# B11 of the merged weight evicted with the turned sign, and eleven x slots in the first stage of a two-layer graph kernel

## The chip, the cores and the metric

The kernel runs on one core of a Trainium2 chip, in fp32. The metric is the device time of one execution in microseconds (us), as the median of several executions. A separate execution is recorded by the hardware profiler; its times count from the start of its span. TensorE multiplies matrices, VectorE (DVE) and ScalarE (ACT) work element by element, GpSimd (POOL) does small operations and issues the stores here, and SyncE (SP) issues most loads.

## The reference

Two layers over a graph of N = 3327 nodes with D = 512 features. `x` is [3327, 512] and `adj` is a dense [3327, 3327] matrix:

```
h = relu(layernorm(x))
q, k, v = h @ Wq.T + bq, h @ Wk.T + bk, h @ Wv.T + bv
a = q @ k.T / sqrt(D) + adj + adj
x = x + softmax(a) @ v

h = relu(layernorm(x))
A2 = adj + eye(N)
dscale = diagonal(A2) ** -0.5
x = x + relu((dscale[:, None] * A2 * dscale[None, :]) @ (A2 @ h @ W.T))
```

## The kernel before, in words

The rows are padded to 3328, that is 26 row tiles of 128 (`NT`), paired as t and t + `HALF` (13 pairs). Wq and Wk are merged into one matrix M = Wq' Wk / sqrt(D), so that the scores are h M h' and k is never formed. All large products are done as a Strassen-Winograd scheme of seven block products in place of eight. For such a product the right operand is kept as four blocks and four combinations: `four_differences(b)` (line 177) makes b[4] = b[0] - b[1], b[5] = b[3] + b[4], b[6] = b[1] - b[3] and b[7] = b[2] - b[5], all on VectorE. b[0] itself is needed with its sign turned, so a negation of b[0] follows it.

The **first stage** (lines 266 to 380) is what the change touches:

- The loads: wq and the later x tiles are issued by SP, wk and three early x tiles by ScalarE's queue. `load_x` (line 272) takes the next slot of `x_ring` (line 269), a ring of SBUF slots, seven of them before. A slot is free again when the tile's normalised copy has been written.
- M: sixteen matmuls (line 305) into four PSUM banks, then eight copies with a scale by ScalarE (line 309), two column halves of each bank, into the blocks M[0] to M[3]; M[0] is made of the left halves of the first two banks. Then come the four differences on VectorE (lines 179 to 182) and the negation of M[0] on ScalarE (line 312), which has to wait until line 179 has read M[0].
- Each x tile, in `h_transposed` (line 314): BNStats and its aggregate on VectorE (`norm`, lines 193 to 197), the power -1/2 on GpSimd (line 199), a bias on VectorE (line 203), then h by a ScalarE activation (line 321), which frees the x slot. GpSimd stores h (line 322). TensorE transposes it in four blocks into one PSUM bank (line 325); the banks are used in turn, two of them. The bank of a tile of the lower half (i < HALF) is emptied by a ScalarE copy (line 328); that of a tile of the upper half by a ScalarE copy (line 330) and two VectorE additions (lines 331 and 332), which also form the combinations of the left operand in `hp`. The tiles of a pair follow each other. After a group of pairs two more additions (lines 333 and 334) form the rest.
- A small product of wk with the bias (line 371, 32 one-column matmuls) follows the first group's transposes in the text.
- `project_q` (line 336) then forms the queries from M and `hp`: chains of matmuls (line 345) whose results are taken out by ScalarE (line 350, the first value) and VectorE (line 353, what is added to it), and stored by GpSimd (line 360).

The instruction order of this stage is set by the framework's scheduler, which works from the program's text, data dependences and buffers; each engine then runs its list in order. In the order so built, the transposes of the first group stand among the products of the one before, and the first two loads of `adjT` blocks (line 416, 384 KB each), which belong to the next stage, stand on SP between the seventh and the eighth x tile. From the scores (line 452) on, the order is written out by hand.

The SBUF slots called `mid` are shared over the stages: 0 to 3 hold h tiles in the first stage (`n_ring`, line 270); in the score stage 0 to 7 hold adjacency blocks (`g_rings`), 8 and 9 sums of them (`o_ring`), 10 and 11 and 13 and 14 other sums.

Of the kernel before, what the change touches and what calls it, by code (L numbers as in the profile page):

```python
# [12 lines left out]
ALU = mybir.AluOpType  # L13
# [34 lines left out]
def graph_layers_kernel(  # L48
# [28 lines left out]
    nc = tc.nc  # L77
# [4 lines left out]
    scale = 1.0 / math.sqrt(D)  # L82
    E = D // 2
# [25 lines left out]
    def bank(k, name):  # L109
        return banks.tile([P, BW], F32, name=name, tag=f"bank{k}")  # L110

    def ring(*slots):

        turn = itertools.cycle(slots)

        def take(shape, name):
            kind, k = next(turn)
            return kind(k, shape, name)

        return take  # L120
# [53 lines left out]
        nc.vector.tensor_add(o[:, 2], o[:, 1], g[:, 0])  # L174
        nc.vector.tensor_add(o[:, 3], o[:, 2], g[:, 2])  # L175

    def four_differences(b):

        yield nc.vector.tensor_sub(b[4], b[0], b[1])
        yield nc.vector.tensor_add(b[5], b[3], b[4])  # L180
        yield nc.vector.tensor_sub(b[6], b[1], b[3])
        yield nc.vector.tensor_sub(b[7], b[2], b[5])
# [83 lines left out]
                Chain.before()  # L266
            Chain.before = None

    x_ring = ring(*((mid, k) for k in range(10, 15)), (half, 13), (half, 14))
    n_ring = ring(*((mid, k) for k in range(4)))  # L270

    def load_x(i, queue=nc.sync):
# [6 lines left out]
    def blocks(slots, name):  # L279

        return [b[:, k] for b in (half(j, [P, 2, 2, E], name) for j in slots) for k in range(2)]
# [3 lines left out]
    first = {}  # L285
# [7 lines left out]
    M = blocks(range(4, 8), "M")  # L293
# [8 lines left out]
    ps = [bank(k, "mm") for k in range(DC)]  # L302
# [3 lines left out]
                             start=c == 0, stop=c == DC - 1)  # L306
    for r in range(DC):
        for z in range(2):
            nc.scalar.mul(M[2 * (r // 2) + z][:, r % 2], ps[r][:, z * E : (z + 1) * E], scale)
    for _ in four_differences(M):  # L310
        pass
    nc.scalar.mul(M[0], M[0], -1.0)

    def h_transposed(k):

# [84 lines left out]
    def more_queries(n, qt):  # L400

        wd = Q[groups[n][0]]
        qt += [half(k, [P, 2, Q[0]], "qt")[:, :, :wd] for k in q_slots[n % 2][4:]]
        for _ in four_differences(qt):
            yield
        nc.scalar.mul(qt[0], qt[0], -1.0)
        yield
# [142 lines left out]
    with in_order(*(e.engine for e in (nc.vector, nc.tensor, nc.gpsimd, nc.sync))):  # L550
# [9 lines left out]
        k = len(steps)  # L560
# [144 lines left out]
    class Right:  # L705
# [31 lines left out]
        def make(self):  # L737
            own, r = self.own, self.r
            if r == "p5":
                nc.vector.tensor_sub(own, self.two[:, :, 0:E], self.two[:, :, E:D])  # L740
            if r == "p6":
                nc.vector.tensor_add(own, own, self.two[:, :, 0:E])
                nc.vector.tensor_sub(own, own, self.two[:, :, E:D])
                nc.gpsimd.dma_start(self.t2[:, 0 : 2 * self.n], self.b[:, 0 : 2 * self.n])
            if r in ("p7", "p4"):
                nc.vector.tensor_sub(own, own, self.one)
            if self.n == 2:
                for _ in four_differences([self.b[:, k] for k in range(8)]):
                    pass
# [187 lines left out]
    def number_of(g, r, s, t):  # L937
        return ((g * len(ORDER) + r) * 2 + s) * len(every) + t
# [5 lines left out]
    for g in range(3):  # L944
        for n, r in enumerate(ORDER):
            for t, e in enumerate(every):
                k = number_of(g, n, 0, t)
# [9 lines left out]
    for n, job in enumerate(jobs):  # L957
        k = k0 + n * (k1 - k0) // len(jobs)
# [17 lines left out]
    for g in range(2):  # L976
        k = number_of(g, 5, 1, 2)
# [6 lines left out]
    for (n, s, t), its in {  # L984
# [4 lines left out]
        for i, when in zip(its, (between, within)):  # L989
            if i is not None:  # L990
                k = number_of(2, n, s, t)
# [428 lines left out]
```

## Time and profile before

| what | value |
|---|---|
| time, median of 5 executions | 2215.72 us (2214.07 to 2220.13) |
| the profiled execution: its own time | 2218.74 us |
| its span | 2217.0 us |
| its mean granted TensorE clock | 0.994 |
| TensorE busy in the span | 2178.9 us (98%) |
| ScalarE, at the negation (line 312), ahead of the last two M evictions: wait for VectorE | 4.78 us, ended 24.59 |
| x tiles 1 to 7 landed | 8.07 to 14.23 us |
| x tiles 8 to 11 issued, landed | 15.30 to 17.41, 18.16 to 22.59 us |
| x tiles 12 to 15 issued, landed | 27.25 to 31.54, 30.05 to 36.46 us |
| the last x tile landed | 61.17 us |
| first score product (line 452) | 122.0 us |

The table is read like this. The span is the profiled execution as the hardware recorded it; its own time lies 1.7 us above the span and 3.0 us above the median. TensorE's busy share says that it is at work nearly all the time. The three rows on x tiles come from following each load from its issue to its landing: between 17.41 and 27.25 SP issues no x tile. The granted clock of TensorE is full except for 24.35 to 31.18, 1997.25 to 2004.08, the start, and the tail from 2205.47 on, where it is half.

### The profile page before, as it was taken

To read this page: it belongs to the slowest core of one execution; us is meant where nothing else is said; L and a number is where in the kernel's file an instruction comes from. 1 tells how busy PE (TensorE), PEld (TensorE's weight loads), DVE (VectorE), ACT (ScalarE), POOL (GpSimd) and SP (SyncE) were. 2 spreads that over 40 slices of the span, in tenths; PEclk is the share of its full clock that TensorE was granted. 3 is DMA by queue.
4 is the path that set the end of the run, shared out by engine and by line. 5 is a ranking of instruction groups with operands and counts; after the bars stand their busy time and mean duration, and the time that the engine had idled before them with its cause. 6 is when DMAs were issued, how large, how long until landed. Compare 5 with 4: busy or idle time off the path is not lost.

```text
span 2217.0 us, 20976 instructions
## 1 busy us (share of the span) xinstructions
PE 2178.9 (98%) x6268; PEld 1167.7 (53%) x6268; DVE 1627.9 (73%) x3103; ACT 231.6 (10%) x336; POOL 356.1 (16%) x551
## 2 busy tenths in 40 slices
PE   9999999999999999999999999999999999999997
PEld 5555555455545555555454555555545555555554
DVE  6369888888877788877777778886645358776776
ACT  5312111211110000000001000000000000000011
POOL 4223333333331000001222100000000000000001
PEclk9999999999999999999999999999999999999998
DMA  7658888888969898788787999876645458765685
GB/s 250 213 203 299 293 302 284 299 285 310 351 208 322 308 371 310 273 295 310 259 304 262 312 340 355 281 275 200 215 140 188 131 185 305 236 201 178 208 302 170
DMA packets 246682, 583.68 MB, mean 263 GB/s; under 512 B 34768, under 2 KB 106270, under 8 KB 246558
## 3 DMA queue, kind: packets, MB, share of 16 engines
q1 hardware_dynamic: 192270, 399.28, 54.3%
q0 software_dynamic: 44928, 167.49, 19.9%
q10 hardware_dynamic: 9360, 15.47, 2.2%
q8 instruction: 52, 0.85, 0.2%
q14 instruction: 72, 0.59, 0.1%
HBM read 414.28 MB, written 167.85 MB: 263 GB/s over the span
## 4 chain that ended last, share of the span: by engine, by line
PE 89%; DVE 4%; DMA 3%; issue 2%; POOL 0%; ACT 0%; SPq 0%; ACTq 0%; POOLq 0%; DVEq 0%
PE p L780 53%; PE Y L452 12%; PE p L872 8%; PE Z L452 6%; PE p L772 5%; PE X L452 3%; PE Y L345 2%; DMA xt<-in_x_dram 1%; DMA g<-in_adjT_dram 1%; PE Z L345 1%; DVE part L173 1%; PE pt L925 0%; PE X L345 0%; DMA xr<-x1d 0%; DVE part L174 0%
## 5 line engine op out<-in xcount | busy, mean ns | idle before, releaser
L780 PE MATMUL p<-part,b 128*128 128x448 f32 (+1 forms) x3528 | 1255.0, 514 | 6.1 <-DVE part L174 4.9
L780 PEld LDWEIGHTS p<-part,b 128*128 128x128 f32 x3528 | 669.1, 190 | 571.4 <-issue 309.0
L173 DVE TENSOR_TENSOR part<-part 128x896 f32<-128x896 f32 (+1 forms) x252 | 257.0, 1020 | 93.5 <-PE p L780 48.6
L452 PE MATMUL Y<-qt,hp 128*128 128x448 f32 (+1 forms) x832 | 309.3, 514 | 4.8 <-DVE g L456 3.8
L452 PEld LDWEIGHTS Y<-qt,hp 128*128 128x128 f32 x832 | 157.0, 190 | 140.9 <-issue 72.3
L452 PE MATMUL Z<-qt,hp 128*128 128x384 f32 (+1 forms) x416 | 162.6, 513 | 0.0
L175 DVE TENSOR_TENSOR part<-part,part 128x448 f32<-128x448 f32 (+1 forms) x219 | 129.5, 591 | 16.6 <-DVE part L174 0.5
L174 DVE TENSOR_TENSOR part<-part,part 128x448 f32<-128x448 f32 (+1 forms) x219 | 129.4, 591 | 7.4
L772 PE MATMUL p<-part,b 128*128 128x448 f32 (+1 forms) x336 | 124.2, 513 | 0.0
L872 PE MATMUL p<-w,ct 128*128 128x512 f32 x272 | 123.5, 593 | 0.5 <-DVE part L884 0.4
L452 PEld LDWEIGHTS Z<-qt,hp 128*128 128x128 f32 x416 | 78.8, 190 | 67.4 <-issue 37.3
L456 DVE SCALAR_TENSOR_TENSOR g<-g,Y 128x384 f32<-128x384 f32 (+1 forms) x156 | 91.3, 585 | 29.3 <-PE Y L452 27.2
L866 POOL DMA_DIRECT2D sum<-job x52 | 28.4, 547 | 501.7 <-DVE job L863 283.1
L809 DVE TENSOR_TENSOR part<-p,part 128x384 f32<-128x384 f32 (+1 forms) x33 | 19.3, 586 | 107.9 <-PE p L780 107.1
L772 PEld LDWEIGHTS p<-part,b 128*128 128x128 f32 x336 | 63.6, 190 | 53.7 <-issue 32.4
L808 ACT COPY part<-p 128x384 f32<-128x384 f32 (+1 forms) x33 | 16.6, 502 | 683.4 <-PE p L780 682.4
L872 PEld LDWEIGHTS p<-w,ct 128*128 128x128 f32 x272 | 51.5, 190 | 59.8 <-issue 51.9
L452 PE MATMUL X<-qt,hp 128*128 128x384 f32 (+1 forms) x208 | 81.1, 513 | 0.0
L459 ACT ACTIVATE g<-g 128x768 f32<-128x768 f32 (+1 forms) x48 | 43.0, 896 | 354.4 <-DVE g L456 300.5
L444 POOL DMA_DIRECT2D sum<-o x52 | 36.9, 709 | 222.1 <-DVE o L438 151.9
L872 PE MATMUL p<-w,part 128*128 128x512 f32 x144 | 65.7, 592 | 0.0
L92 POOL DMA_DIRECT2D out_dram<-r x30 | 16.2, 542 | 305.3 <-DVE r L928 270.2
(166 smaller groups left out, 1879.1 us busy)
## 6 DMA issues: line engine op xcount, KB each, us to landing
part<-sum SPq DMA_DIRECT2D x104, 448.0 KB, 4.9
part<-p SPq DMA_DIRECT2D x91, 448.0 KB, 6.3
part<-sum SPq DMA_DIRECT2D x104, 384.0 KB, 3.5
part<-p SPq DMA_DIRECT2D x91, 384.0 KB, 4.1
part<-in_adjT_dram SPq DMA_DIRECT2D x78, 448.0 KB, 4.7
b<-row SPq DMA_DIRECT2D x234, 128.0 KB, 4.9
part<-in_adjT_dram SPq DMA_DIRECT2D x78, 384.0 KB, 3.8
g<-in_adjT_dram SPq DMA_DIRECT2D x52, 448.0 KB, 4.7
```

The costliest lines, as they stand in the source:

```text
L173: nc.vector.tensor_add(o[:, 0:2], g[:, 0:4:3], g[:, 1:2].to_broadcast([P, 2, g.shape[-1]]))
L174: nc.vector.tensor_add(o[:, 2], o[:, 1], g[:, 0])
L175: nc.vector.tensor_add(o[:, 3], o[:, 2], g[:, 2])
L345: nc.tensor.matmul(ps[:, :w], M[B[name]][:, c, o * P : (o + 1) * P], hp[k][:, A[name], c], start=start and c == 0, stop=c == 1, skip_group ...
L444: nc.gpsimd.dma_start(self.to(sumd)[:, 0:2], self.o)
L452: nc.tensor.matmul(ps[:, :wd], h_of(self.t, name, k), qt[B[name]][:, k], start=start and k == 0, stop=k == 1, skip_group_check=True)
L456: nc.vector.scalar_tensor_tensor(a[n], a[n], 2.0, ps[:, :wd], op0=ALU.mult, op1=ALU.add if sign > 0 else ALU.subtract)
L459: nc.scalar.activation(g[1], g[1], AF.Exp, **({"bias": pad} if self.t == HALF - 1 else {}))
L772: yield nc.tensor.matmul(ps[("p2", "p3", "p4", "p8")[k]][:, :w], b[:, z], a[:, 0, y], start=k == 3, stop=True)
L780: yield nc.tensor.matmul(ps[r][:, :w], b[:, i], m, start=self.t == 0, stop=self.t == PAIRS - 1 and r in ("p1", "p5", "p6", "p7"))
L866: nc.gpsimd.dma_start(sumd[self.s][self.j][:, 2 + self.k], self.a)
L872: nc.tensor.matmul(ps, cts[s][y][d][:, k * P : (k + 1) * P], w[d], start=d == 0, stop=d == DC - 1)
```

## The change

`four_differences` gets an argument with which it leaves out b[4]. The ring of x slots takes four slots more, `mid` 6 to 9, and so has eleven. The two evictions that form M[0] are scaled by -scale, so that M[0] is written with its turned sign at once. M[4] = M[0] - M[1] is then made from the turned block in one VectorE instruction, (M[0] * -1) - M[1], ahead of the other three differences, which don't read M[0]. The separate negation on ScalarE is gone.

```diff
-    def four_differences(b):
-
-        yield nc.vector.tensor_sub(b[4], b[0], b[1])
+    def four_differences(b, first=0):
+
+        if first == 0:
+            yield nc.vector.tensor_sub(b[4], b[0], b[1])
         yield nc.vector.tensor_add(b[5], b[3], b[4])
...
-    x_ring = ring(*((mid, k) for k in range(10, 15)), (half, 13), (half, 14))
+    x_ring = ring(*((mid, k) for k in range(6, 15)), (half, 13), (half, 14))
...
-            nc.scalar.mul(M[2 * (r // 2) + z][:, r % 2], ps[r][:, z * E : (z + 1) * E], scale)
-    for _ in four_differences(M):
+            turned = -scale if r < 2 and z == 0 else scale
+            nc.scalar.mul(M[2 * (r // 2) + z][:, r % 2], ps[r][:, z * E : (z + 1) * E], turned)
+    nc.vector.scalar_tensor_tensor(M[4], M[0], -1.0, M[1], op0=ALU.mult, op1=ALU.subtract)
+    for _ in four_differences(M, 1):
         pass
-    nc.scalar.mul(M[0], M[0], -1.0)
```

No further line differs. "Rows used one a step in another order", in the short description of the change, has no line of its own: the order changes only as the scheduler builds it from these edits. In the order so built:

| engine | what stands differently |
|---|---|
| ScalarE | eight M evictions in a row; before, the negation stood between the sixth and the seventh |
| VectorE | M[4] stands behind the BNStats of the 15th x tile; before, behind that of the 11th; the additions of the first pair (lines 331, 332) follow the differences of M in both |
| SP | the first adjacency load stands behind x tile 11, the second behind tile 15; before, both stood ahead of tile 8 |
| GpSimd | the powers (line 199) stand a little earlier among the stores of h |
| TensorE | three neighbouring groups change places (products of line 345 and transposes) |
| all, from the scores on | the same |

## The prediction

> **What bounds the kernel now.** I read the page's totals first, then TensorE's waits in the first stage, its timeline, and windows for the transfers and the clock. All times are us from the span's start; tiles of x are counted in the order of their loads.
>
> ```profile
> PE 2178.9 (98%) x6268; PEld 1167.7 (53%) x6268; DVE 1627.9 (73%) x3103; ACT 231.6 (10%) x336; POOL 356.1 (16%) x551
> ```
>
> TensorE is idle for 2217.0 - 2178.9 = 38.1 us in all. The change keeps the count and shapes of the matmuls, so it can only move idle time or the time in which the clock is halved. It edits the first stage alone, and behind that stage the two programs' instruction orders are the same on every engine. So only TensorE's gaps up to the first score product (L452, 122.0) count:
>
> ```profile
> PE tp L325 <- ACT hp L328: 2.7, 2, 2.0
> PE tp L325 <- DVE hp L332: 2.2, 2, 1.7
> PE Z L345 <- DVE hp L331: 0.9, 1, 0.9
> PE Y L345 <- ACT qs L350: 0.8, 1, 0.8
> PE tp L325 <- ACT ht L321: 0.2, 1, 0.2
> ```
>
> (The columns are total us, times, longest.) They sum to 6.8 us, which is the most that removed waits can bring. The first is the wait that the change aims at. The timeline shows its cause:
>
> ```profile
> 23.88 0.68 DVE L179 TENSOR_TENSOR M<-M 128x512 f32<-128x512 f32 x1
> 24.59 0.63 ACT L312 ACTIVATE M<-M 128x512 f32<-128x512 f32 x1 [4.78 <-DVE M L179]
> ...
> 25.66 0.59 ACT L328 COPY hp<-tp 128x512 f32<-128x512 f32 x1
> ...
> 26.30 1.12 PE L325 MATMUL tp<-ident,ht 128*128 128x128 f32 x4 [1.98 <-ACT hp L328]
> ...
> 27.94 0.41 DVE L332 TENSOR_TENSOR hp<-hp,tp 128x256 f32<-128x256 f32 x1
> ...
> 28.09 1.97 PE L325 MATMUL tp<-ident,ht 128*128 128x128 f32 x8 [0.68 <-ACT hp L328]
> ```
>
> The reader is to see a chain. ScalarE stands at the negation of M[0] (L312), which waits for M[4] on VectorE (L179), which stands behind the BNStats of the 11th x tile (landed 22.59). Behind L312 queue the last two M evictions and the copy that empties the first transpose bank, so TensorE has no bank from 24.3 to 26.30, then again for 0.68. The later gaps have x tiles behind them:
>
> ```profile
> 36.19 0.91 PE L345 MATMUL Z<-hp,M 128*128 128x384 f32 x2 [0.88 <-DVE hp L331]
> ...
> 62.69 0.63 PE L325 MATMUL tp<-ident,ht 128*128 128x128 f32 x4 [1.75 <-DVE hp L332]
> ```
>
> In the first, L331 (35.73) stood behind a BNStats whose tile landed at 35.10; in the second, L332 (62.13) stood behind two whose tiles landed at 60.09 and 61.17. Between 22.59 and 30.05 no x tile lands at all: all seven slots are full and ScalarE, which frees them (L321), is stuck.
>
> **The change part by part.**
>
> *The turned sign and the missing negation.* ScalarE loses one 0.63 us instruction and a 4.78 us wait. All eight evictions now follow one another: the sixth ended at 19.81, two more take about 0.65, so L328 of the first tile runs when its transposes are done (about 20.9) and ends near 21.5. Tile 3's transposes then start when TensorE is through with its bias products, at 24.31, not 26.30: **1.99 us earlier**. The next four, for tile 5 in the same bank, move with them (28.09 to 26.10). They end at 27.08 at the half rate of these records (1.97 for eight, so 0.98 for four).
>
> *M[4] as a scalar_tensor_tensor.* It takes the place of one tensor_sub of 0.68. The nearest row is L884, the same kind on 128x512 reading PSUM, 0.75; the other end is 0.68. I take 0.68; the 0.07 does not show.
>
> *Eleven slots.* Four more x tiles are loaded before any slot is freed. The program order on SP changes: x tiles 8 to 11 go ahead of both adjacency loads (384 KB each, issued at 10.63 and 11.12 before), the first of these follows tile 11, the second tile 15; no later instruction needs them before 87 us. Tiles 12 to 15, issued at 27.25 to 31.54 before, now wait for the first four slots, freed when tiles 8 to 11 were issued before (15.30 to 17.41). On VectorE there is a price: M[4], and with it L331/L332 of the first pair, stand behind the BNStats of the **15th** tile in place of the 11th. Queued behind it are the other three differences and these two additions; waiting for them is TensorE, for the second bank (tile 4).
>
> So when does tile 15 land? The windows of the transfers and of the clock:
>
> ```profile
> core 0: us, PE busy (x) PEld busy (x) DVE busy (x) ACT busy (x) POOL busy (x), PEclk, DMA share, GB/s
> 17.30:23.20 5.90, 5.90 (x39) 4.42 (x37) 3.21 (x12) 2.06 (x7) 2.89 (x6) 1.00 0.85 324
> ...
> 20.94:24.35 3.41, 3.37 (x31) 3.29 (x30) 2.28 (x10) 0.00 (x0) 0.00 (x0) 1.00 0.46 179
> 24.35:27.77 3.42, 1.12 (x4) 0.72 (x4) 2.18 (x5) 2.95 (x7) 0.25 (x1) 0.50 0.00 0
> 27.77:31.18 3.41, 3.09 (x10) 2.41 (x11) 1.75 (x7) 2.91 (x6) 2.40 (x5) 0.50 0.63 196
> ...
> 1997.25:2000.67 3.42, 2.35 (x4) 1.28 (x5) 3.32 (x8) 0.47 (x1) 0.00 (x0) 0.50 0.61 227
> ```
>
> At 16.29 before had landed all its early loads, 0.79 MB of adjacency among them. After has four x tiles and one adjacency block in their place, 1.44 MB; the extra 0.65 MB costs 2.0 us at 324 GB/s, so this lot is in at about 18.2. Then come four x tiles and four row stores (L322), 2.1 MB or 6.5 us: 24.7 for the last of them. In before the last of these eight was a store, 0.62 behind the last tile (23.21 against 22.59), so tile 15 lands at about **24.0**. Here the Trainium skill bears (DMA: Bandwidth & Descriptors, "Anatomy of one DMA"): a fixed 2.0 us plus bytes over 436 GB/s. By that rate the extra costs 1.5 and the lot 4.8, and tile 15 is in near 22.0; L332 would then be done before TensorE wants the bank, and the front gain would be the full 1.99. The row, taken with reads and stores mixed, decides: 324. The page's section "Issuing engines are not separate DMA queues" warns in the same direction: transfers of all issuers interleave on 16 engines, so more slots bring no bandwidth, only an earlier start. The trace has room for one: the row at 24.35 shows a DMA share of 0.00.
>
> From the landing, by the distances of before: 0.98 from that BNStats to M[4], 0.61 for each of M[4] and three differences, 0.33 to L332, 0.41 for it: 24.0 + 0.98 + 2.44 + 0.33 + 0.41 = 28.1. Tile 4's transposes start at 28.1 against 29.07 (28.09 + 0.98): **0.97 us is gained at the front**, not 1.99. That is one us for each us of tile 15, nought at a landing of 25.0.
>
> From there x tiles are issued four tiles earlier. Tiles came some 1.6 us apart (27.25 to 55.72 for 15 of them is 1.9), so 6 us or more of lead stands against waits of 1.75 at the most. So the gaps at 36.19 (0.88), 54.52 (0.15), 57.94 (0.42) and 62.69 (1.75) go: **3.20 us**. What is late next is the drain by ScalarE and VectorE; VectorE was busy 9.25 of 10 between 40 and 50, where TensorE did not wait. The 0.78 at 100.2 waits for L350, not for x, and stays.
>
> *The clock.* The half rate at 24.35 to 31.18 lies in before although TensorE was busy 3.37 of the 3.41 ahead of it: those are the bias product's one-column matmuls, which after has too. The Trainium skill (TensorE: Matmul & The Clock Gate, "What's actually happening") lets a free-running 3.4 us window decide, idle to half, busy to full. If after's window from 24.35 counts as busy, full rate returns at 27.77 and about 1.6 us more is gained (3.1 us of work at half rate). But after fills it with only 1.12 + 0.98 = 2.1 of 3.41, and the row at 1997.25 had 2.35 and left the clock at half. So by the row: no gain. The next window, 28.1 to 31.18, has 3.08, as 3.09 before, and is enough. If L332 ends later than 28.8 it holds under 2.35, and the half rate lasts to 34.6: up to 1.7 lost.
>
> *The slots' later use.* The slots added now hold x until the last L321, near 79; the adjacency and sum tiles that share them are written from 84 on (VectorE L438 at 87.85). The cover is 5 us or more; each us beyond it would cost up to one.
>
> **Sum.** 0.97 + 3.20 = 4.2 us. Against the profiled execution, 2218.74, that is 2214.5; the median before, 2215.72, is 3.0 lower, and I subtract from it: **2211.5**.
>
> **Rivals.**
> - *Everything fits* (0.15): tile 15 lands by 23, nothing waits at 27, the clock comes back early. 1.99 + 3.20 + 1.6 = 6.8: 2208.9. For it: share 0.00 in the middle of the stall. Against it: 324 GB/s.
> - *A new wait in the old one's place* (0.22): tile 15 lands at 25 to 26.5, L332 ends at 29 to 30.6. The front gives 0 to -1.5, the clock loses up to 1.7; with 3.20 later the sum is between +3 and 0: about 2214. For it: VectorE's order, and reads that meet stores.
> - *Slower* (0.13): transfers move at 236 GB/s (the last column), as in a later window of the same stage:
>
> ```profile
> 40.00:50.00 10.00, 10.00 (x38) 6.11 (x37) 9.25 (x32) 6.06 (x11) 5.59 (x10) 1.00 0.71 236
> ```
>
>   From 15.3 some 3.0 MB are left, tile 15 lands at 28, tile 4 starts at 32.1: 3.0 lost, clock 1.7 lost, and if row stores hold back the later tiles too, only half of the 3.20 comes: 3.1 slower, 2218.8. It decides from a landing of tile 15 near 27.
> - *No effect* (0.05): the x gaps return because stores, not slots, set the pace of loads (tile 14 was issued right at a store's landing, 30.57): within 1 of 2215.7.
>
> The forecast's own case has 0.45 and a range of 2209.5 to 2213.5. The range for 8 in 10 runs from 2207.0 to 2217.3, with the medians' own scatter (2214.07 to 2220.13). A measurement of this kernel tells some 0.2% (4.4 us) from no change, and 4.2 lies just at that bound: of the forecast's case I give half to each side. Faster by over 0.2%: 0.23 + 0.14 + 0.05 of luck in the phase of the clock's windows, 0.42. Slower by over 0.2%: that rival with a second clock window lost (another 1.7), 0.07, and 0.05 for the same luck the other way: 0.12. Within: 0.46.
>
> **What would show it.** Right: no ScalarE wait between the evictions; tile 3's transposes at 24.3; tile 15 landing near 24 and L332 ending near 28; no TensorE gap at 36, 58 or 62; L452 starting near 118. Wrong: tile 15 landing after 26, half rate past 31.2, or VectorE still waiting for x after 40.

## The result, and the profile after

| | before | after |
|---|---|---|
| median of the timed executions | 2217.58 us (44, 2213.78 to 2221.93) | 2212.62 us (23, 2206.51 to 2217.66) |
| profiled execution, its span | 2217.0 us | 2208.2 us |
| ratio after to before | | 0.9978, 95% interval 0.9972 to 0.9985 |

The change makes the kernel 4.9 us faster (0.0022 of 2217.6; by the interval 3.3 to 6.2). 4.2 were forecast. From here on a gain "by time" is 1 minus the ratio, times 2217; the difference of two medians can lie 1 us beside it. The spans of the two profiled executions differ by more, 8.8 us, and most of that is not the change. I cut each trace at the end of the merged weight's matmuls (line 305 before, 306 after) and at the first score product (line 452, 454): 19.97 and 121.86 before, 18.67 and 117.44 after. So 1.3 us lie ahead of the end of these matmuls (the last section says what this end goes with), 3.1 in the first stage behind it, and 4.4 behind the stage, where nothing is edited.

The page's totals of after:

```profile
PE 2175.5 (99%) x6268; PEld 1167.0 (53%) x6268; DVE 1627.6 (74%) x3103; ACT 230.9 (10%) x335; POOL 357.1 (16%) x551
```

TensorE's idle time is 2208.2 - 2175.5 = 32.7 us, against 38.1. Its waits between 20 and 130 in after (total us, times, longest):

```profile
PE Y L347 <- ACT qs L352: 1.1, 1, 1.1
PE tp L327 <- DVE hp L334: 0.9, 1, 0.9
PE tp L327 <- ACT hp L330: 0.7, 1, 0.7
PE tp L327 <- DVE nb L204: 0.7, 1, 0.7
```

They sum to 3.4 us; before they were 6.8. The wait of 2.0 for ScalarE's copy is gone, and so is the wait for VectorE's addition at 61 (1.75). One wait is new at the front, for L334. The one at 54.5, put down to L204, stands ahead of the 18th group of transposes, as the 0.42 of before at 57.94 does. The timeline of after around the front:

```profile
21.99 0.68 DVE L194 BATCH_NORM_STATS2 st<-xt 128x6 f32<-128x512 f32 x1
22.59 0.67 DVE L312 SCALAR_TENSOR_TENSOR M<-M 128x512 f32<-128x512 f32 x1
22.87 0.64 PE L327 MATMUL tp<-ident,ht 128*128 128x128 f32 x4
...
23.54 0.58 ACT L330 COPY hp<-tp 128x512 f32<-128x512 f32 x1 [2.72 <-PE tp L327]
...
24.18 0.87 PE L327 MATMUL tp<-ident,ht 128*128 128x128 f32 x4 [0.68 <-ACT hp L330]
...
25.51 0.41 DVE L334 TENSOR_TENSOR hp<-hp,tp 128x256 f32<-128x256 f32 x1
...
25.98 1.11 PE L327 MATMUL tp<-ident,ht 128*128 128x128 f32 x4 [0.94 <-DVE hp L334]
```

ScalarE has no negation to stand at; it waits for TensorE now. M[4] (L312) comes right behind the BNStats of the 15th tile, which landed at 21.78, and the first pair's last addition, L334, behind the differences. TensorE stands 0.94 us for it: this is the wait that takes part of the old one's place. Of the prediction's signs of being right, those of the front came, all a little earlier than named (tile 3's transposes at 22.87, the 15th tile at 21.78, L334's end at 25.92), and the gaps at 36 and 62 are gone; the one at 58 is not. Of its signs of being wrong, the half rate reaches just past 31.2 (31.32), and VectorE waits for no x tile after 40.

### The profile page after: what moved, and what is told of

Same layout as the page of the kernel before. It is cut to its first block, busy times and chain, and to the rows that moved or that the text cites. A ratio compares the mean times of both kernels' runs of the same rounds, so it can differ in the third digit from the quotient of the medians.

```text
span 2208.2 us, 20973 instructions
## 1 busy us (share of the span) xinstructions
PE 2175.5 (99%) x6268; PEld 1167.0 (53%) x6268; DVE 1627.6 (74%) x3103; ACT 230.9 (10%) x335; POOL 357.1 (16%) x551
## 4 chain that ended last, share of the span: by engine, by line
PE 87%; DVE 4%; issue 3%; DMA 3%; POOL 1%; ACT 0%; SPq 0%; ACTq 0%; POOLq 0%; DVEq 0%
PE p L782 52%; PE Y L454 12%; PE p L874 7%; PE Z L454 6%; PE p L774 5%; PE X L454 3%; PE Y L347 1%; DMA xt<-in_x_dram 1%; DMA b<-row 1%; DVE part L173 1%; PE pt L927 0%; DMA p<-g 0%; DVE part L174 0%; DMA xr<-x1d 0%; PE tot L507 0%
```

## The experiments

A single profile says little here, since the same kernel's gaps differ from one execution to the next. So the kernel before, the changed kernel and each of its two parts were profiled twice. In this table, d is the time from the end of the merged weight's matmuls to the first score product; idle is the part of it in which no matmul ran; clock is half of the matmul time that fell into stretches of half clock, that is, about what the half clock cost.

| kernel | d | idle | clock | windows of 3.41 at half rate | ratio to before (95%) |
|---|---|---|---|---|---|
| before | 101.9, 101.1 | 6.6, 4.1 | 2.1, 4.3 | 2, 3 | |
| after | 98.8, 96.8 | 3.4, 1.5 | 3.0, 3.1 | 2, 2 | 0.9978 (0.9972 to 0.9985), 0.9978 (0.9968 to 0.9988) |
| sign alone | 98.5, 101.4 | 3.0, 4.0 | 3.1, 4.8 | 2, 3 | 0.9988 (0.9979 to 0.9997), 0.9989 (0.9979 to 0.9999) |
| slots alone | 101.9, 100.9 | 5.0, 4.3 | 4.4, 4.1 | 3, 3 | 0.9987 (0.9980 to 0.9994), 0.9990 (0.9981 to 0.9999) |
| M first | 96.7, 98.3 | 1.4, 2.8 | 3.1, 3.1 | 2, 2 | 0.9969 (0.9957 to 0.9981), 0.9979 (0.9970 to 0.9989) |
| wide bias | 100.3 | 5.7 | 1.7 | 1 | 0.9987 (0.9980 to 0.9994) |
| M first, wide bias | 97.9 | 4.5 | 0.0 | 0 | 0.9970 (0.9958 to 0.9982) |
| M first, split bias | 95.1 | 2.2 | 0.0 | 0 | 0.9973 (0.9963 to 0.9983) |
| the same, queries later | 94.5 | 2.0 | 0.0 | 0 | 0.9972 (0.9960 to 0.9984) |

Idle time and clock can stand in for each other: where the half rate falls into the bias product, that product takes longer and TensorE comes later to the wait behind it. So the second profile of before has 2.6 us less idle time than the first, but 2.2 more lost to the clock, and d is only 0.8 shorter.

### Each part alone

Theory: the sign takes away ScalarE's stall at the front, the slots take away the later waits for x tiles, and the two add up. Rival: both cure one lack, loads of x that don't start while ScalarE is stuck, so either alone brings nearly everything. The sign alone is the changed kernel with

```diff
-    x_ring = ring(*((mid, k) for k in range(6, 15)), (half, 13), (half, 14))
+    x_ring = ring(*((mid, k) for k in range(10, 15)), (half, 13), (half, 14))
```

and the slots alone are the kernel before with the opposite edit. Expected of the sign alone:

> The turned sign and the scalar_tensor_tensor, with seven x slots as before (M[4] stands behind the BNStats of the 11th tile again). If the two parts add up, this gives the front alone: tile 3's transposes 2 us earlier, tile 4's about 1 us earlier, and the gaps at 36, 58 and 62 that wait for x stay: about 1.0 us faster than before, ratio 0.9995. Rival, that the parts cure the same lack (no x tile is loaded while ScalarE is stuck, so freeing ScalarE alone lets the loads run 4 us earlier): the later x gaps go too, about 3.5 us faster, ratio 0.9984.

Again, beside the changed kernel:

> The turned sign alone once more (seven slots), for a second profile and beside e7 on one chip. Idle up to the first score product 3.0 us with the 1.8 us gap at 58 if what e1 showed is no chance; time within 0.5 us of e7 if the slots add nothing on top of the sign, 2 us above it if they do.

> The changed kernel once more, for a second profile and beside e8 on one chip. Additive parts: 2 us faster than e8 (the slots take the 0.42 and 1.75 us waits for late x tiles). Substitutes: within 0.5 us of e8. TensorE idle up to the first score product 3.4 us, as in the first profile.

TensorE's waits between 20 and 125 in the first profile of the sign alone:

```profile
PE tp L327 <- DVE hp L334: 2.2, 2, 1.8
PE tp L327 <- ACT hp L330: 0.7, 1, 0.7
```

The 2.2 us are the gaps at 55 and 58 (0.42 and 1.80; in the second profile 0.42 and 1.69), the 58 and 62 of before. They stay without the slots, and no wait for L334 stands at the front: there M[4] is behind the 11th BNStats, and L334 is in time. Both profiles of the changed kernel have one gap of 0.67 instead, at the place of the first. Only the second of the two waits for a late x tile. VectorE in before, ahead of the first and then of the second:

```profile
56.46 0.16 DVE L203 SCALAR_TENSOR_TENSOR nb<-mv,rstd 128x1 f32<-128x1 f32 x1 [2.09 <-POOL rstd L199]
```

```profile
60.11 0.69 DVE L193 BATCH_NORM_STATS2 st<-xt 128x6 f32<-128x512 f32 x1 [1.25 <-DMA xt<-in_x_dram]
```

By time the sign alone is 2.7 and 2.4 us faster than before, and on one chip the changed kernel's median is 3.0 us below that of the sign alone (2212.58 against 2215.59; 2.4 by the two ratios). The 1.0 us that the theory gave the sign were missed: what was measured lies between this and the rival's 3.5. The 3.4 us of idle time expected of the changed kernel's second profile were missed as well (1.5).

Expected of the slots alone:

> Eleven slots with the separate negation kept (before's M code). If the parts add up: the x gaps go (2.3 us by the trace of after) but ScalarE still stands at the negation until M[4], which now comes behind the 15th BNStats: the front is not earlier, or up to 1 us earlier as tile 15 landed at 21.8; 2.3 to 3 us faster, ratio 0.9988. Rival, the parts cure the same lack: nearly all of the change's gain, 4 us or more, ratio 0.9981.

Again:

> Eleven slots alone once more, for a second profile and more times. Additive parts: 2.8 us faster than before, 2 us slower than the changed kernel. Idle up to the first score product 5 us, and a half rate of two windows instead of the three of e2 if the third there was chance.

TensorE's waits between 20 and 125 in the first profile of the slots alone:

```profile
PE Y L345 <- ACT qs L350: 1.5, 1, 1.5
PE tp L325 <- ACT hp L328: 1.4, 2, 0.8
PE tp L325 <- DVE hp L332: 1.3, 1, 1.3
PE tp L325 <- DVE nb L203: 0.7, 1, 0.7
```

Of the gaps at 58 and 62 only 0.67 is left, at the place of the first, but the front keeps its wait for ScalarE's copy (0.77, and 1.45 in the second profile; 1.98 and 0.90 in the two profiles of before) and a wait at 36 (1.34 and 0.77). This one has a late x tile behind it, with eleven slots:

```profile
34.94 0.69 DVE L193 BATCH_NORM_STATS2 st<-xt 128x6 f32<-128x512 f32 x1 [2.29 <-DMA xt<-in_x_dram]
...
36.43 0.63 PE L325 MATMUL tp<-ident,ht 128*128 128x128 f32 x4 [1.34 <-DVE hp L332]
```

The sign alone has no gap there, and VectorE in it waits for no x tile between 33 and 57. With the slots alone no x load is issued from 16.53 to 25.86, where ScalarE stands at the negation and frees no slot. So the lateness near 35 goes with ScalarE's stall and not with the number of slots: here the rival is right. By time the slots alone are 2.9 and 2.2 us faster than before. Three windows at half rate, in place of the two expected, came in the second profile too.

So some 2.5 for the sign, 2.2 to 2.9 for the slots, and 4.9 for both: the times favour the parts that add up. Each interval is about 2 us wide to either side, so the rival's 3.5 for one part alone is not excluded by one run, but the 3.0 us between the changed kernel and the sign alone on one chip speak against it, and so do the gaps: the wait for the negation and the lateness near 35 go with the sign, the wait for x near 60 with the slots. The length of the stage does not show it. By the means of two profiles d is 101.5 before, 100.0 with the sign, 101.4 with the slots and 97.8 with both: the slots' idle time is 0.7 us less than before, but the half clock took 1.0 us more. Over the timed runs it does not: their mean granted clock (0.9943 and 0.9946) is that of before beside them (0.9945 and 0.9943). Where the slots' 2.2 to 2.9 us lie is therefore not shown by these profiles.

### Which gaps were there by chance

> The kernel before once more, for a second profile. If its first-stage gaps are those of its order: idle 6 to 7 us up to the first score product with the gaps of 2.0 at 24, 0.7, 0.9 at 36 and 1.75 at 61; two or three windows at half rate. If they are chance, the places differ by over 1 us.

In the second profile of before the gaps at 24 (0.90), 26 (0.68), 56 (0.41) and 60 (1.72) stand at their places, and the one at 36 (0.88 in the first) is absent, though nothing was changed. It was a gap of that execution. The 2.0 at 24 also has a chance part: 0.90 here, where the half rate began at 22.61 inside the bias product and this product took 4.21 us in place of 3.63. The expectation of 6 to 7 us idle was missed: 4.05.

### The new wait: M first

If the wait for L334 is what is left of the old stall, putting M[4] to M[7] and the first pair's additions ahead of the 12th tile's BNStats should remove it. On the changed kernel, with an order-only dependence on VectorE:

```diff
+            rstd, bias = norm(xt, stats_behind) if j > 11 else norm(xt)
...
+        for ins in ahead:
+            tc.add_manual_dep(nc.cur_bb.bb.instructions[-1], ins.name,
...
```

where `ahead` holds the four M instructions and line 334's instruction of the second tile, and `stats_behind` is called right after a BNStats is issued.

> The changed kernel, with M[4] to M[7] and the first pair's two additions put ahead of the BNStats of the 12th x tile on VectorE (order only). If the new wait behind the 15th BNStats is what is left of the old one, the 0.94 us gap at tile 4's transposes goes (the 0.68 us wait for ScalarE's copy stays): 0.9 us faster than the changed kernel, 5.5 to 6 than before, and up to 1.6 more if TensorE's window from 24.3 then counts as busy and the clock comes back at 27.8. Rival, that delaying four BNStats starves the later transposes: no gain, ratio as the changed kernel, 0.9978.

> M first once more, as e3 had six times only. If the wait behind the 15th BNStats costs what the first profile of the changed kernel showed (0.94), 1 us faster than the changed kernel, ratio to before 0.9973 to 0.9965; if it is mostly absent, as in the second profile, the changed kernel's time.

The wait for L334 at the front is gone in both profiles. But it is gone in the second profile of the changed kernel too, where the bias product ran partly at half clock (4.64 us instead of 3.63) and tile 3's transposes later and slower (1.09 instead of 0.64), so that L334 at 25.45 was in time for 26.5. On average this order gains nothing that its 16 runs can show beside the changed kernel: medians 2212.05 and 2212.39 against 2212.62 and 2212.58. So the new wait costs between 0 and 0.94 us, and is not worth an edit of its own.

### The half clock at the front

All of these kernels but those with a changed bias product fall to half clock within 2 us of that product's end or in the middle of it. Its 32 matmuls have one column each. To see whether their width matters, each was made 128 columns wide by repeating the column, in the changed kernel:

```diff
-            nc.tensor.matmul(pu[:, r : r + 1], w_k[c // 2][:, c % 2, r * P : (r + 1) * P], bq_sb[:, c : c + 1],
+            nc.tensor.matmul(pu[:, r * P : (r + 1) * P], w_k[c // 2][:, c % 2, r * P : (r + 1) * P],
+                             bq_sb[:, c : c + 1].to_broadcast([P, P]),
...
-    nc.vector.tensor_scalar(u, pu[:, :DC], scale, None, op0=ALU.mult)
+    nc.vector.tensor_scalar(u, pu[:, ::P], scale, None, op0=ALU.mult)
```

> The changed kernel with each of the one-column matmuls of the bias product made 128 columns wide (the column repeated), the same count. If the half clock from 24.4 comes from these matmuls being counted as little activity, it goes: TensorE works at full rate from 24 on, 2 us faster than the changed kernel or a little less where other engines then set the pace, ratio to before 0.9970. If the clock goes by TensorE being busy at all, the half rate stays, and the wider matmuls cost nothing to 1 us more: ratio 0.9978 to 0.9983.

The ratio was 0.9987, by this slower than the changed kernel, and the run settles nothing by itself: the scheduler put transposes in the middle of the product, and TensorE then stood 2.96 us for L334. One window at half rate followed that gap. So the product was held in one block, by an order-only chain on TensorE from the first three tiles' transposes through it, on top of M first:

> e3_m_first with the bias product's matmuls 128 columns wide and held in one block at the place of before (behind the second tile's transposes), so that only their width differs up to there. If width sets the clock's count of activity: full rate through the block and behind it, no half rate in the first 60 us, 2 to 3 us faster than e3, ratio 0.996. If not: half rate from the window that lies in the block, as in before, and e3's time or 1 us more, ratio 0.997 to 0.9975.

Windows that lie in this product, in M first and then in M first with the wide product (window, TensorE busy, weight loads, VectorE, ScalarE, GpSimd, granted clock, DMA share, GB/s):

```profile
core 0: us, PE busy (x) PEld busy (x) DVE busy (x) ACT busy (x) POOL busy (x), PEclk, DMA share, GB/s
19.61:23.02 3.41, 3.41 (x33) 3.41 (x32) 3.31 (x12) 1.82 (x5) 1.23 (x2) 1.00 0.98 360
23.02:26.43 3.41, 2.73 (x14) 2.33 (x14) 1.72 (x5) 1.30 (x2) 0.00 (x0) 0.50 0.38 141
26.43:29.84 3.41, 3.41 (x10) 2.21 (x9) 1.29 (x9) 2.97 (x5) 2.56 (x5) 0.50 0.69 164
```

```profile
19.99:23.41 3.42, 3.42 (x33) 3.42 (x32) 3.32 (x7) 2.30 (x5) 1.39 (x3) 1.00 0.96 316
23.41:26.82 3.41, 2.00 (x17) 1.52 (x15) 2.98 (x13) 2.47 (x5) 1.39 (x3) 1.00 0.71 272
```

In both, TensorE is busy through the whole first window. With one column per matmul the clock then halves for two windows; with 128 it stays full, even through a window with 2.00 of 3.41 busy. The ten profiles with the one-column product in one piece all fall to half rate in it or within 2 us of its end, this one does not: width counts, not being busy alone. But the time of M first with the wide product (0.9970) is that of M first (0.9969 and 0.9979): what the clock gave, TensorE then waited out for the other engines (idle 4.5 us against 1.4 and 2.8, with single gaps of 1.68 and 1.31). The timed runs say the same. The mean granted clock of the 7 runs with the wide product is 0.9963, against 0.9942 for the 11 of the changed kernel on the same chip, which is worth about 4.7 us of the span; yet the medians are 2212.49 and 2212.58.

How long the half rate lasted hung in two profiles on the 0.68 us wait for ScalarE's copy. Second profile of the changed kernel, then the second of the sign alone; both fell to half rate at 21.7:

```profile
25.09:28.50 3.41, 2.95 (x10) 2.41 (x11) 1.97 (x11) 2.91 (x6) 1.36 (x3) 0.50 0.29 109
```

```profile
25.12:28.53 3.41, 2.73 (x11) 2.02 (x11) 2.23 (x8) 2.82 (x6) 1.16 (x2) 0.50 0.27 74
28.53:31.94 3.41, 3.41 (x10) 2.09 (x9) 2.18 (x10) 1.93 (x4) 3.29 (x6) 0.50 0.79 268
```

The same wait of 0.68 began at 24.87 in the first, so that part of it fell ahead of the window, and at 25.18 in the second. 2.95 of 3.41 (86%) brought the clock back, 2.73 (80%) didn't, and a third window at half rate cost the second kernel 1.7 us (its clock column is 4.8 against 3.1). This is part of how the two profiles of the sign alone differ by 2.9 us in d.

### An attempt at a faster version

If the product's one-column matmuls are mixed with transposes, both the half clock and the 0.68 wait could go. On top of M first, in `h_transposed`, with an order-only chain on TensorE over the first five tiles and the product, and the differences of M issued behind the first pair's additions (the step that takes the product's result out of PSUM is held behind the additions of tile 4):

```diff
+            if 2 <= j <= 5:
+                bias_of(j - 2)
```

> On top of e3_m_first, orders alone: the bias product in four parts between the transposes of tiles 3, 4, 5 and the first product, and the first pair's two additions ahead of M[4]. If the 0.68 us wait for ScalarE's copy is a matter of there being nothing to do meanwhile, it goes; and if the half clock comes from 3.6 us of one-column matmuls in a row, mixing them with transposes leaves the clock full or shortens the half rate (3.1 us of e3's TensorE time is lost to it). 2 to 4 us faster than e3, ratio to before 0.996 to 0.995. Rival, the clock falls all the same: 0.7 us faster than e3, ratio 0.9966.

The clock is full from 5.59 to 1988.7, and all of the front's gaps over 0.2 us are gone. What is left of the stage's gaps is 1.30 at 48 and 0.67 at 93. The latter waits for ScalarE's line 352 (L392 in this kernel), which stands behind a ScalarE instruction on the first query difference of VectorE; that difference had waited 7.78 us for its load. It was put behind the additions that it held up (`adds` are the instructions of after's line 355 in the text's order):

```diff
-    for _ in more_queries(0, coming):
-        pass
+    queries_0 = more_queries(0, coming)
+    next(queries_0)
+    behind(adds[17])
+    for _ in queries_0:
+        pass
```

> On top of e5_split_bias, the first difference of the query blocks put behind the two additions to qs that it held up (order only). If the 0.67 us wait of TensorE at 93 is that difference's wait for its load, it goes: 0.7 us faster than e5, ratio to before 0.997 or a little less, with the clock full up to the first score product again. Rival, the difference is then late for the scores: a gap of the same size comes at the first score product.

TensorE's waits between 20 and 125 in it:

```profile
PE tp L358 <- ACT ht L354: 1.9, 2, 1.4
```

The 0.67 is gone and nothing comes up at the first score product; left are the gap at 48 (1.38) and a new 0.55 at 21.7. d is 94.5, the shortest of all, 3.2 below the changed kernel's mean of 97.8. The medians are 2212.71 for the first version (12 runs) and 2210.93 for the second (6 runs). Both beat the kernel before clearly. Against the changed kernel the times show no gain: on the first version's chip it stands at 2212.58, and the intervals of both versions (0.9963 to 0.9983 and 0.9960 to 0.9984) overlap with its own. The 2 to 4 us expected over M first were missed. The stage is shorter in one profile of each version; that the kernel is faster is not shown.

## Why the prediction was right

The time, 2212.62, lies 1.1 us from the forecast of 2211.5, against a median of before that was itself 1.9 higher in the larger sample. The gain is 4.9 where 4.2 were forecast. That the two lie so close is in part luck: the waits that the sum named gave 3.0 us, and places that it put at nothing the rest. By its steps, each against the mean of two profiles before and two after:

- *The front, 0.97.* The gaps ahead of 30 were 2.66 and 1.58 before, and 1.62 and 0.68 after: 0.97 on the mean. The mechanism was as told, ScalarE's stall out and VectorE's order in, with tile 3's and tile 5's transposes early and tile 4's behind L334. Both ends were smaller than in the sum: the old stall was 1.98, 0.90, 0.77 and 1.45 in the four profiles that have it, the new wait 0.94 or nothing. That 0.97 was forecast and 0.97 measured is chance: counted as the sum counts it, by the start of tile 4's transposes behind the merged weight's end, the gain is 1.7 in the first pair of profiles and 0.6 in the second.
- *Tile 15 at 24.0.* Counted from the end of the merged weight's matmuls that is 4.0; it was 3.1 and 3.2. The early lot was in at 17.12, 18.4 on before's scale, where 18.2 was forecast. The term that was off is the rate of the eight transfers behind it: 2.1 MB from 17.12 to the last row store at 22.58 are 384 GB/s, not 324. The row of before that I took it from had an idle end in it: 370 GB/s from 17.30 to 22.30 and 68 from there to 23.20. The Trainium skill's 436 GB/s (DMA: Bandwidth & Descriptors, "Anatomy of one DMA") was too fast by about as much as the row was too slow; the page fits it to loads that GpSimd issues, and here SP issued the four x tiles. From the landing to L334's end it took 4.14, where 4.1 were forecast.
- *The gaps at 36 and 54.5, 1.03.* They were 1.03 in one profile of before and absent in the other. On the mean some 0.5 was there to gain. To read a gap as the kernel's own from one profile was a step that failed; its cause in that execution, a tile landing at 35.10, was real. The other failure is the cure: the prediction gave this gap to the slots, but with the slots alone it stands (1.34 and 0.77), and with the sign alone it is absent.
- *The gaps at 58 and 62, 2.17.* The one at 62 (1.69 to 1.80) is in all four profiles with seven slots and in none with eleven, so the slots remove it, as told. The one at 58 (0.41 or 0.42) is no wait for x: VectorE waits for no x tile between 36 and 60 in before; it stood 2.09 us for GpSimd's power, and the pair's additions came late. With eleven slots it is 0.67 (0.55 in M first, and nothing in the last two kernels). The profile puts the 0.67 down to L204, which ends 0.07 us behind the pair's last addition, L334; why it grew was not tested. Together 1.5 is gained.
- *The 0.78 at 100, nought.* 0.78 and 0.24 before, 1.08 and 0.00 after.
- *The clock, nought.* Two windows at half rate in both profiles of after, two and three in those of before. The argument from the window of 69% that was not enough held: the window from 24.49 in after has 73% (2.48 of 3.41) and left the clock at half. Windows of 80 and 82% did so too, and one of 81% did not (last section), so the 69% were not the limit.

These steps make 0.97 + 0.5 + 1.5 = 3.0 us of idle time; d as a whole fell by 3.7 (101.5 to 97.8, means of two). The rest up to 4.9, some 1.2 us, would lie behind the first score product. There the two profiles of before took 2081.2 and 2082.0 us to their last matmul, and those of after 2076.8 and 2081.1. The places that differ are waits of the score stage for adjacency loads at 570 to 610 and whether one or two windows near 1995 run at half clock. Both vary within one kernel by as much as between them. Over all fourteen profiles this stretch takes 2078.4 us on the mean with eleven slots (ten profiles, 2075.8 to 2081.5) and 2081.0 with seven (four, 2077.9 to 2083.0). That hints at a gain of the slots behind the stage, where the prediction has none, but the ranges overlap and no cause was tested, so it stays open.

## What to carry to other kernels

An operation that stands between an engine's evictions and waits for another engine is best folded into the evictions, but look at what the scheduler then does with the other engine's order: here more early loads let four more statistics slip ahead of the one result that TensorE needed. Profile a kernel twice before you build a sum on gaps under 1 us: of 6.6 us idle in the first profile, 2.6 were absent in the second, and most of that had become matmul time at half clock. And where the time won lies inside a stretch at half clock, or just ahead of other engines' work, expect part of it back only: M first with the wide product had no half rate to pay for in this stage, and waited 4.5 us instead.

## What the runs showed of the hardware

- The clock's count of activity is not the busy time of the records. A window full of one-column matmuls (3.41 of 3.41 busy) was followed by half rate, the same window with 128 columns was not. What share of it they make matters: with TensorE busy throughout, a window with 2.25 us of them lost the clock (second profile of the sign alone, from 18.29), ones with 2.22 (split bias, from 19.24) and 1.69 (after, from 17.66) kept it. The Trainium skill (TensorE: Matmul & The Clock Gate, "What's actually happening") speaks of idle and busy windows of about 3.4 us; the length is what these traces show (3.41), but which window counts as which is not told by TensorE's busy share.
- The busy share gives no sharp limit for other matmuls either. At half rate, windows with 69% (2.35 of 3.42), 80% (2.73 of 3.41) and 82% (2.80 of 3.42, second profile of before) left the clock low, one with 86% (2.95 of 3.41) raised it, but so did one with 81% (2.78 of 3.41, after, from 1990.57). At full rate a window with 59% (2.00 of 3.41) kept it, and one with 41% (1.39 of 3.41, before, from 1993.84) lost it; between them one with 43% kept it (1.48 of 3.41, queries later, from 872.03) and one with 47% lost it (1.60 of 3.42, second profile of after, from 1987.75). So it took more to raise the clock than to keep it, in these traces about 80% against somewhat under half.
- The windows' place against the start differs from run to run: the clock first rose at 4.01 to 7.28 us in the profiles of this study, and the merged weight was done at 18.57 to 19.97. The two go together: a rise at 4.01 to 4.64 goes with an end at 18.57 to 18.74, one at 7.28 with 19.97. That is 1.3 us of the 8.8 between the first two profiles.
